# Attention of a gated cross-attention and mixture-of-experts block: its tensor engine products in a written order, and the queries of four groups by quarters, seven products in place of eight

## The chip, the cores and the metric

The kernel runs on one core of a Trainium2 chip. The metric is the device time of one execution in microseconds; the median of three runs is compared. TensorE is called PE here (its weight loads PEld), VectorE DVE, ScalarE ACT, GpSimd POOL; SyncE (SP) issues most of the DMA.

## The reference

The input `x` has 4 x 1024 rows of 256 numbers, the context 4 x 64 rows. All is float32.

```python
def attention(q, k, v):                       # q: normalised x; k, v: the context
    qh = einsum('bld,hdk->hblk', q, w_qs)     # 16 heads of 64
    kh = einsum('bld,hdk->hblk', k, w_ks)
    vh = einsum('bld,hdk->hblk', v, w_vs)
    attn = softmax(einsum('hblk,hbmk->hblm', qh, kh))
    out = einsum('hblm,hbmk->hblk', attn, vh) * qh
    return out.transpose(1, 2, 0, 3).reshape(...) @ w_proj.T + b_proj

def ffn(xt):                                  # 8 experts, the best 2 of each token
    logits = einsum('td,ed->te', xt, gate_w)
    weights = softmax(top_2(logits))          # 0 for the experts not chosen
    h = silu(einsum('td,edf->tef', xt, w1))   # 256 -> 1024
    y = einsum('tef,efd->ted', h, w2)         # 1024 -> 256
    return einsum('ted,te->td', y, weights)

x = x + tanh(g_xattn[0]) * attention(layernorm(x), ctx, ctx)
x = x + tanh(g_ffn[0]) * ffn(layernorm(x))
```

## The kernel before

**Groups and steps.** The 4096 rows are eight groups `g` of 512 (two to a batch, `GB`), a group four tiles of 128 (`T`). The main loop runs over `g` from 0 to 8 and, inside, over four steps `t`. Step `t` of turn `g` works on three groups at once:

- of group `g`: the scores of tile `t` against the keys of the batch (`sc`, 8 products) and the softmax, in `probabilities`. DVE takes the row maximum (`mx`) and subtracts it, ACT exponentiates, DVE sums (`sm`) and inverts, POOL multiplies. One step later `transpose_probabilities` turns the tile with 8 transposes on PE (`pa`), and ACT copies it to `aT`;
- of group `g + 1`: its queries (`pq`), eight pairs of heads spread over the steps by the table `parts`. `queries` multiplies, for each pair, two 128-row blocks of `wq` by 512 columns of the normalised, transposed rows `nT`, and ACT copies the sum from its bank in PSUM to `qT`;
- of group `g - 1`: at step 1 `attend` multiplies attention by values (`po`, four banks for half of the heads), and DVE multiplies by the query in `qT`. At steps 2 and 3 `project` makes the output projection (`pp`, 16 products each), which DVE adds to `x` (line 493).

**Norms.** `ln_stats` and `ln_norm` make the first norm for group `g + 2`: DVE normalises four tiles (line 312), PE turns them (`pt_a`), ACT copies them to `nT`. `add_bias` is on POOL.

**Routing.** After every second group `after` does one part a step for the two groups finished: statistics of the second norm (step 0), norm and logits of the first group (step 1) and of the second (step 2), `route` (step 3), and `place` at step 0 of the next turn. `logits` is a chain: transposes `pt_b`, products `pl` with the gate, a copy to SBUF by DVE, one transpose `pl_t`, a copy to `lg` by DVE (line 520). `route` is some 35 small DVE instructions from `lg` on: comparisons (lines 531 to 536), `chosen` (540), and eight running sums `prior` (543, 544), one for each tile. `place` multiplies `chosen` and `prior` on PE (`prow`, lines 565 and 566); the rows found go to DVE and, through scatters by POOL (`enter`), into a table in DRAM. The rounds belong to groups 0 and 1 (routed at turn 3), 2 and 3 (turn 5), 4 and 5 (turn 7), and 6 and 7 (after the loop).

**Experts.** `run_slots` works through slots of 256 to 384 tokens of one expert: hidden layer (`ph`), output (`py`), a scatter-add into the output. Nine early slots serve groups 0 to 3 and begin inside the loop, by the table `pieces`; the late ones need a table that is made after the last round. `hidden_by_quarters` and `pair_of_blocks` already use seven products for eight in some slots.

**What sets the order.** A scheduler orders each engine's instructions; those given to `pinned` keep the order in which the program states them. Before the change, in attention, that is only the start. Each engine then runs its own list in order and waits at semaphores. PSUM has four single banks (`bank`, pool `ps1`) and two double ones for scores and hidden layers (`ps2`). Large tiles in SBUF come from pools of equal blocks: seven are called `weight`.

Of the kernel before, what the change touches and what calls it, by code (L numbers as in the profile page):

```python
# [15 lines left out]
P = 128  # L16
# [5 lines left out]
def kernel(  # L22
# [140 lines left out]
    load_wk = load_heads(w_ks, "wk", (nc.scalar, nc.sync), "hidden", parts_of)  # L163
    wk, _ = next(load_wk)
# [115 lines left out]

    def ln_stats(groups, name):
# [16 lines left out]
    def ln_norm(g, stats, name):  # L298
# [10 lines left out]
        for t in range(T):  # L309
# [6 lines left out]
            for c in range(NC):  # L316
                turn = nc.tensor.transpose(
                    pt[c][:, t * P : (t + 1) * P], xn[:, c * P : (c + 1) * P], ident
                )
                pinned(turn, first)  # L320
# [50 lines left out]
    def values(ctxT):  # L371

        n = 512 // P
        for b0 in range(0, B, 2):
            for p0 in range(0, NP, n):
                pv = bank(f"pv_{b0}_{p0}")
                for c in range(NC):
                    nc.tensor.matmul(
# [25 lines left out]
    def queries(g, qT, pairs):  # L404
        for p in pairs:
            pq = bank(f"pq_{g}_{p}")
            for c in range(NC):
# [7 lines left out]
                pinned(product, (g, p, c) == (0, 0, 0))  # L415
            nc.scalar.copy(of_pair(qT, p), pq)  # L416

    newest = []

    def probabilities(g, t, qT):  # L420

        sc = ps2.tile([P, NP // 2, 2, 2, M], F32, tag="ps2", name=f"sc_{g}_{t}")
        for p in range(NP):
            nc.tensor.matmul(  # L424
# [23 lines left out]
    def transpose_probabilities(g, t, pr, aT):  # L448
        prv = pr.rearrange("p (i j) m -> p i (j m)", j=2)
        n = 512 // P  # L450
        for p0 in range(0, NP, n):
            pt = bank(f"pa_{g}_{t}_{p0}")
            for i in range(n):
                nc.tensor.transpose(pt[:, i * P : (i + 1) * P], prv[:, p0 + i, :], ident)  # L454
# [4 lines left out]
    def attend(g, pairs, qT, aT):  # L459

        for q in range(pairs[0] // 2, pairs[-1] // 2 + 1):
# [3 lines left out]
            for r in range(2):  # L465
                for j in range(2):
                    half = slice(j * M, (j + 1) * M)
                    i = q * 2 + r
                    nc.tensor.matmul(  # L469
# [10 lines left out]
    def project(g, qT, t0):  # L480

        pp = bank(f"pp_{g}_{t0}").rearrange("p (t d) -> p t d", d=D)
        for i in range(2):
            t = t0 + i
            for p in range(NP):
                nc.tensor.matmul(  # L486
# [16 lines left out]
    def logits(g, lg):  # L503

        pl = bank(f"pl_{g}")[:, :P]
        for c in range(NC):
            for t in range(T):
                nc.tensor.matmul(
# [7 lines left out]
        nc.vector.tensor_copy(lT, pl)  # L516
        pt = bank(f"pl_t_{g}")[:, :P]
        nc.tensor.transpose(pt, lT, ident)
# [3 lines left out]
        )  # L522

# [37 lines left out]
    def place(groups, routing, name):  # L561
# [3 lines left out]
        nc.tensor.matmul(pr, earlier, chosen.rearrange("p t e -> p (t e)"), start=True, stop=False)  # L565
        nc.tensor.matmul(pr, ones, prior.rearrange("p t e -> p (t e)"), start=False, stop=True)
# [50 lines left out]
    def counts(name):  # L617

        pn = bank(f"pn_{name}")[:, :E]
        nc.tensor.matmul(pn, ones, taken, start=True, stop=True)  # L620
# [642 lines left out]
    def finish(g, step):  # L1263

        qT, aT = held[g]
        if step == 1:
            attend(g, range(NP // 2, NP), qT, aT)
        elif step >= 2:
            project(g, qT, (step - 2) * 2)
# [4 lines left out]
    second = {}  # L1274
    entered = 0
    done = in_use = None

    def after(g, step):
# [5 lines left out]
        elif step == 1:  # L1284
            second["logits"] = scores_of([R, E], f"lg_{g}")
            ln_norm(groups[0], second, "b")
            logits(groups[0], second["logits"])
        elif step == 2:
            for h in groups[1:]:
                ln_norm(h, second, "b")  # L1290
                logits(h, second["logits"])
        elif step == 3:
            second["routing"] = route(second["logits"], f"{g}")
# [31 lines left out]
    value_parts = (2, 1, 1, 0)  # L1325
# [3 lines left out]
    queries(0, qTs[0], range(NP - 2, NP))  # L1329
    for g in range(NG + 1):  # L1330
        attention_ends = g == NG
        if g < NG:
# [5 lines left out]
        for t in range(T):  # L1338
            if t == 0 and g >= 2:
                leave(g - 2)  # L1340
            if g < NG:
                pr = probabilities(g, t, qT)
            if last:
                transpose_probabilities(*last)
# [5 lines left out]
            if g and t == 1:  # L1350
                attend(g - 1, range(NP // 2), *held[g - 1])
            for h, pairs in parts[g].items():
                queries(h, qTs[h], pairs[t])
            if 0 <= g - 1 < NG:
                finish(g - 1, t)
            last = (g, t, pr, aT) if g < NG else None
# [3 lines left out]
            if behind >= 0:  # L1360
                after(ends, behind)
            if g == 0 and t == 1:
# [6 lines left out]
            if g + 2 < NG:  # L1369
                if t == 0 and (g + 2) % GB == 0:  # L1370
                    stats = ln_stats(list(range(g + 2, g + 2 + GB)), f"a{g + 2}")
                elif t == 2:
                    ln_norm(g + 2, stats, "a")
                    add_bias(g + 2)
            if g < 2:
                clear(g * T + t, 2 * T)
            for _ in range(pieces[g][t] if g in pieces else 0):
                next(slots)

    leave(NG - 1)  # L1380
    for step in range(2 * T):
        if step == T:
            placing(NG - 1)
        after(NG - 1, step)
        for _ in range((1, 1, 1, 2, 1, 1, 1, 1)[step]):
# [46 lines left out]
```

## Time and profile before

| | |
|---|---|
| median of three runs | 878.94 us (878.19 to 879.98) |
| the profiled execution's own time | 880.53 us |
| its span | 878.7 us |
| mean granted clock of PE | 0.987 |
| busy: PE, PEld | 842.2, 681.6 us |
| busy: DVE, ACT, POOL | 496.0, 244.6, 265.9 us |
| chain that ended last | PE 77%, DVE 12%, waits for issue 4% |
| attention's last projection ends | 442.8 us |

The product of two float32 operands appears as two records on PE, each with a weight load; a transpose is one record. In rows by group, "x256" counts records. "Idle before" is the time for which the engine had nothing to do just before the instruction, and the name behind it is what ended that. Where a row merges several instructions, its duration runs from the first start to the last end.

### The profile page before, as it was taken

Reading aid. Unit: us, or ns where it says so; the run is one execution under the profiler, and the core shown is the slowest. Engines: PE = TensorE matmul, PEld = TensorE weight load, DVE = VectorE, ACT = ScalarE, POOL = GpSimd, SP = SyncE. Lnnn points to the kernel's source line nnn. Section 1 sums busy time; section 2 is a strip of 40 time slices with the busy share of each in tenths; the row PEclk is TensorE's granted clock in tenths of the full one; section 3 lists DMA queues with packets and bytes.
Section 4 is the critical chain, followed back from the end, with each engine's and each line's share of the span. In section 5 each row is a group of like instructions: output and inputs, shape, how many; then the busy total and the mean of one; then the engine's idle time right before and its main releaser. Section 6 shows DMA issues by size and latency. Waiting matters only on the chain.

```text
span 878.7 us, 13306 instructions
## 1 busy us (share of the span) xinstructions
PE 842.2 (96%) x4684; PEld 681.6 (78%) x4684; DVE 496.0 (56%) x1202; ACT 244.6 (28%) x413; POOL 265.9 (30%) x216
## 2 busy tenths in 40 slices
PE   8999999999999999999999699999999999999996
PEld 5555858485767768785888489899999999899995
DVE  4466384679557966862138443665556753546520
ACT  2663242334332323440112012222222221222210
POOL 3052212223721373207224532123222232222132
PEclk9999999999999999999999699999999999999998
DMA  9999999201100055426675668686667675546611
GB/s 197 336 340 341 340 346 340 85 1 60 61 25 1 25 174 163 108 68 189 165 203 147 173 147 215 164 237 140 144 165 178 157 218 133 133 115 176 184 22 37
DMA packets 165032, 141.79 MB, mean 161 GB/s; under 512 B 72685, under 2 KB 159076, under 8 KB 161248
## 3 DMA queue, kind: packets, MB, share of 16 engines
q1 hardware_dynamic: 145456, 118.79, 46.5%
q0 software_dynamic: 12912, 17.11, 10.1%
q10 hardware_dynamic: 6592, 4.98, 1.8%
q8 instruction: 39, 0.64, 0.3%
q14 instruction: 33, 0.27, 0.1%
HBM read 78.73 MB, written 62.46 MB: 161 GB/s over the span
## 4 chain that ended last, share of the span: by engine, by line
PE 77%; DVE 12%; issue 4%; POOL 2%; ACT 2%; DMA 1%; SPq 0%; POOLq 0%; DVEq 0%; ACTq 0%
PE py L1183 20%; PE ph L955 14%; PE ph L1005 11%; PE pp L486 9%; PE pq L408 8%; PE q L1073 5%; PE sc L424 4%; PE pa L454 2%; DVE mx L433 2%; PE po L469 2%; DVE sm L440 1%; DVE pr L435 1%; DVE qT L478 1%; POOL table L606 1%; POOL pr L443 1%
## 5 line engine op out<-in xcount | busy, mean ns | idle before, releaser
L1146 POOL DMA_INDIRECT out_dram<-x,ids x69 | 108.7, 1575 | 306.8 <-DVE x L1161 102.0
L1183 PE MATMUL py<-w,hT 128*128 128x256 f32 (+1 forms) x960 | 186.0, 362 | 0.0
L1183 PEld LDWEIGHTS py<-w,hT 128*128 128x128 f32 (+1 forms) x960 | 160.0, 181 | 21.6 <-issue 1.7
L955 PE MATMUL ph<-xT,w 128*128 128x256 f32 x576 | 135.9, 390 | 7.2 <-issue 7.2
L955 PEld LDWEIGHTS ph<-xT,w 128*128 128x128 f32 x576 | 111.0, 196 | 26.7 <-issue 12.0
L443 POOL TENSOR_TENSOR pr<-pr,sm 128x1024 f32<-128x1024 f32 x32 | 61.4, 1918 | 208.4 <-DVE sm L441 143.0
L408 PE MATMUL pq<-nT_a,wq 128*128 128x512 f32 x256 | 116.1, 597 | 5.7 <-DVE qT L478 3.9
L486 PE MATMUL pp<-wp,qT 128*128 128x256 f32 x512 | 113.5, 379 | 1.3 <-issue 1.3
L486 PEld LDWEIGHTS pp<-wp,qT 128*128 128x128 f32 x512 | 97.0, 190 | 20.0 <-issue 7.4
L408 PEld LDWEIGHTS pq<-nT_a,wq 128*128 128x128 f32 x256 | 46.2, 190 | 58.2 <-issue 44.0
L963 ACT ACTIVATE hT<-ph 128x1024 f32<-128x1024 f32 (+1 forms) x40 | 37.2, 940 | 192.7 <-PE ph L955 119.3
L606 POOL DMA_INDIRECT table<-x,to_row x64 | 62.5, 976 | 42.7 <-DVE x L595 24.8
L424 PEld LDWEIGHTS sc<-keys,qT 128*128 128x128 f32 x512 | 62.6, 192 | 11.2 <-issue 10.8
L424 PE MATMUL sc<-keys,qT 128*128 128x128 f32 x512 | 67.1, 278 | 0.0
L1161 DVE TENSOR_SCALAR x<-py,ids 128x256 f32<-128x256 f32 (+1 forms) x53 | 24.8, 468 | 69.8 <-PE py L1183 63.8
L455 ACT COPY aT<-pa 128x512 f32<-128x512 f32 x64 | 34.7, 592 | 84.1 <-PE pa L454 74.0
L433 DVE TENSOR_REDUCE mx<-sc 128x16 f32<-128x1024 f32 x32 | 39.0, 1219 | 28.0 <-PE sc L424 27.9
L440 DVE TENSOR_REDUCE sm<-pr 128x16 f32<-128x1024 f32 x32 | 39.0, 1219 | 23.9 <-ACT pr L438 21.5
L478 DVE TENSOR_TENSOR qT<-po,qT 128x512 f32<-128x512 f32 x64 | 40.9, 679 | 13.7 <-PE po L469 9.7
L1019 ACT ACTIVATE hT<-hT 128x384 f32<-128x384 f32 (+1 forms) x66 | 33.1, 501 | 51.1 <-DVE hT L1016 48.2
L416 ACT COPY qT<-pq 128x512 f32<-128x512 f32 x64 | 36.5, 581 | 35.3 <-PE pq L408 34.5
L1005 PE MATMUL ph<-x,sa 128*128 128x192 f32 (+1 forms) x264 | 43.6, 314 | 2.0 <-issue 2.0
(278 smaller groups left out, 999.9 us busy)
## 6 DMA issues: line engine op xcount, KB each, us to landing
w<-in_L_ffn_w_dram SPq DMA_DIRECT2D x58, 1024.0 KB
table<-empty SPq DMA_DIRECT2D x8, 5016.0 KB
x<-table SPq DMA_DIRECT2D x116, 64.0 KB
out_dram<-x ACTq DMA_DIRECT2D x8, 512.0 KB
x<-in_x_dram SPq DMA_DIRECT2D x7, 512.0 KB
out_dram<-x,ids POOLq DMA_INDIRECT x69
wq<-in_L_xattn_w_qs_dram SPq DMA_DIRECT2D x4, 256.0 KB
wv<-in_L_xattn_w_vs_dram SPq DMA_DIRECT2D x2, 512.0 KB
```

The lines of the kernel that those rows point to most:

```text
L408: product = nc.tensor.matmul(pq, wq[:, c, p * P : (p + 1) * P], nT[g][:, c, :], start=(c == 0), stop=(c == NC - 1),)
L424: nc.tensor.matmul(sc[:, p // 2, :, p % 2, :], of_pair(qT, p)[:, t * P : (t + 1) * P], kT[g // GB][:, p, :], start=True, stop=True,)
L433: nc.vector.tensor_reduce(mx, scv, AX.X, ALU.max)
L440: nc.vector.tensor_reduce(sm, pr, AX.X, ALU.add)
L443: nc.gpsimd.tensor_tensor(pr, pr, sm.unsqueeze(2).to_broadcast([P, H, M]), ALU.mult).ins,
L478: nc.vector.tensor_tensor(own, po[j], own, ALU.mult)
L486: nc.tensor.matmul(pp[:, i, :], of_pair(qT, p)[:, t * P : (t + 1) * P], wp[:, p, :], start=(p == 0), stop=(p == NP - 1),)
L606: nc.gpsimd.indirect_dma_start(out=table.rearrange("r (u w) -> (r u) w", w=2), out_offset=bass.IndirectOffsetOnAxis(ap=to_row[:, k, i : i ...
L955: nc.tensor.matmul(ph[:, i, :], a[:, c, f * P : (f + 1) * P], xT[:, c, :], start=(c == 0), stop=(c == NC - 1),)
L1005: nc.tensor.matmul(to[:, f, :], left[:, (f0 + f) * P : (f0 + f + 1) * P], right, start=not onto and f == 0, stop=True, skip_group_check=on ...
L1146: rows_added = nc.gpsimd.indirect_dma_start(out=outf.rearrange("n (h d) -> (n h) d", d=w)[:rows_of], out_offset=bass.IndirectOffsetOnAxis( ...
L1183: product = nc.tensor.matmul(py[t][i * m : (i + 1) * m], hT[f // per_tile][:, f % per_tile, t * P : t * P + m], b[:, f, i * w : (i + 1) * ...
```

## The change

**A written order.** `multiply` and `turn` pin every product and transpose of attention from turn 0 on (`steady`), and the loop's body states a new order: the first half of `attend` ahead of the step's scores, the second half after `pa` of the tile before; `pa` itself behind the queries and the projection; the first norm of group `g + 2` at step 3. `logits` becomes a generator in three parts: transposes `pt_b` when it is made, `pl` behind the next step's scores, `pl_t` behind that step's projection.

**Queries by quarters.** For groups 1, 2, 3 and 5, `queries_by_quarters` replaces `queries`. The weights and rows are cut in halves along the contraction and along rows or heads, and seven products of sums replace eight, in two chunks of 14 products of 256 columns (first pairs 0 and 2; a chunk gives two pairs of each half). A chunk uses all four banks, three of them twice. The sums cost four DVE instructions for the weights, once, and four for the rows of each group; five additions a chunk are on DVE, two copies on ACT.

```diff
+    sums_of_wq = block([P, 4, NP // 2 * P], "sums_of_wq", "weight")
+    sums_of_x = block([P, 4, G // 2], "sums_of_x", "weight")
...
+    def multiply(*args, **kwargs):
+        pinned(nc.tensor.matmul(*args, **kwargs), steady)
+    def turn(*args):
+        pinned(nc.tensor.transpose(*args), steady)
...
-                pinned(turn, first)
+                pinned(turned, first or steady)
...
+    QUARTERS = (1, 2, 3, 5)
+    def quarters(h):
+        w = [[wq[:, c, f * NP // 2 * P : (f + 1) * NP // 2 * P] for f in range(2)] for c in range(NC)]
+        x = [[nT[h][:, c, t * G // 2 : (t + 1) * G // 2] for t in range(2)] for c in range(NC)]
+        return w, x
+    def query_weight_sums():
+        w, _ = quarters(0)
+        sa = sums_of_wq
+        for out_, in0, in1, op in (
+            (sa[:, 0], w[0][1], w[1][1], ALU.add),
+            (sa[:, 1], sa[:, 0], w[0][0], ALU.subtract),
+            (sa[:, 2], w[0][0], w[0][1], ALU.subtract),
+            (sa[:, 3], w[1][0], sa[:, 1], ALU.subtract),
+        ):
+            nc.vector.tensor_tensor(out_, in0, in1, op)
+    def query_row_sums(h):
+        _, x = quarters(h)
+        sx = sums_of_x
+        for out_, in0, in1 in (
+            (sx[:, 0], x[0][1], x[0][0]),
+            (sx[:, 1], x[1][1], sx[:, 0]),
+            (sx[:, 2], x[1][1], x[0][1]),
+            (sx[:, 3], x[1][0], sx[:, 1]),
+        ):
+            nc.vector.tensor_tensor(out_, in0, in1, ALU.subtract)
+    def queries_by_quarters(h, qT, f0):
+        w, x = quarters(h)
+        sa, sx = sums_of_wq, sums_of_x
+        per = 2
+        q = [bank(f"pq_{h}_{f0}_{i}").rearrange("p (f n) -> p f n", f=per) for i in range(4)]
+        u2, u3 = (rows.tile([P, per, G // 2], F32, tag="xT", name=f"u_{h}_{f0}_{i}") for i in range(2))
+        to = [[qT[f][:, f0 : f0 + per, t * G // 2 : (t + 1) * G // 2] for t in range(2)] for f in range(2)]
+        def product(to, left, right, onto=False):
+            for f in range(per):
+                multiply(to[:, f, :], left[:, (f0 + f) * P : (f0 + f + 1) * P], right,
+                    start=not onto and f == 0, stop=True, skip_group_check=onto or f > 0)
+        def plus(to, of, other):
+            nc.vector.tensor_tensor(to, of, other, ALU.add)
+        product(q[0], w[0][0], x[0][0])
+        nc.scalar.copy(u2, q[0])
+        product(q[1], sa[:, 1], sx[:, 1])
+        plus(u2, q[1], u2)
+        product(q[2], sa[:, 2], sx[:, 2])
+        plus(u3, q[2], u2)
+        product(q[3], sa[:, 0], sx[:, 0])
+        plus(to[1][1], q[3], u3)
+        product(q[0], w[1][0], x[1][0], True)
+        nc.scalar.copy(to[0][0], q[0])
+        product(q[2], w[1][1], sx[:, 3], True)
+        plus(to[1][0], q[2], u2)
+        product(q[3], sa[:, 3], x[1][1], True)
+        plus(to[0][1], q[3], u2)
...
         nc.vector.tensor_copy(lT, pl)
+        yield
         pt = bank(f"pl_t_{g}")[:, :P]
-        nc.tensor.transpose(pt, lT, ident)
+        turn(pt, lT, ident)
...
-        elif step == 2:
-            for h in groups[1:]:
-                ln_norm(h, second, "b")
-                logits(h, second["logits"])
+        if step in (1, 2):
+            ln_norm(groups[step - 1], second, "b")
+            to_route.append(logits(groups[step - 1], second["logits"]))
...
+    for g in range(NG - 1):
+        if g + 1 in QUARTERS:
+            parts[g] = {g + 1: ([0], [2], [], [])}
-    value_parts = (2, 1, 1, 0)
+    value_parts = (1, 0, 2, 1)
...
+            if g and t == 1:
+                attend_half(g - 1, 0)
             if g < NG:
                 pr = probabilities(g, t, qT)
-            if last:
-                transpose_probabilities(*last)
+            logits_part()
...
             if behind == T:
                 placing(ends)
-            if g and t == 1:
-                attend(g - 1, range(NP // 2), *held[g - 1])
             for h, pairs in parts[g].items():
-                queries(h, qTs[h], pairs[t])
-            if 0 <= g - 1 < NG:
-                finish(g - 1, t)
-            last = (g, t, pr, aT) if g < NG else None
+                if pairs[t]:
+                    ask(h, qTs[h], pairs[t])
+            for _ in range(pieces[g][t] if g in (NG - 1, NG) else 0):
+                next(slots)
+            if g and t >= 2:
+                project(g - 1, held[g - 1][0], (t - 2) * 2)
...
-            if behind >= 0:
+            logits_part()
+            to_route.clear()
+            if 1 <= behind <= 2 and t == 2:
                 after(ends, behind)
+            if g + 2 < NG and t == 3:
+                ln_norm(g + 2, stats, "a")
+                add_bias(g + 2)
+                sum_rows(g + 2)
+            if last:
+                transpose_probabilities(*last)
+            last = (g, t, pr, aT) if g < NG else None
+            if behind >= 0 and not (1 <= behind <= 2 and t == 2):
+                after(ends, behind)
+            if g and t == 1:
+                attend_half(g - 1, 1)
```

`placing` and `prow` keep their place in the program, behind the scores of step 0 and ahead of that step's queries; being products of `multiply`, they are now held there.

## The prediction

> **What bounds the kernel now.** I read the page's first two parts, then the tensor engine (PE) and the vector engine (DVE) in order of time, and then the changed kernel's instruction order on each engine.
>
> ```profile
> PE 842.2 (96%) x4684; PEld 681.6 (78%) x4684; DVE 496.0 (56%) x1202; ACT 244.6 (28%) x413; POOL 265.9 (30%) x216
> L408 PE MATMUL pq<-nT_a,wq 128*128 128x512 f32 x256 | 116.1, 597 | 5.7 <-DVE qT L478 3.9
> ```
>
> PE is busy 96% of the span, and attention (about 30 to 442 us) is no exception: whatever leaves PE there shortens the kernel, and whatever makes PE wait lengthens it. The second row is the query product that the change rewrites; its 5.7 us of idle time is PE waiting behind the attention output `po` for DVE to empty its banks.
>
> Now PE and DVE at the end of group 3, where the first two groups are routed:
>
> ```profile
> 189.41 0.27 PE L518 MATMUL pl_t<-ident,lT 128*128 128x128 f32 x1
> ...
> 191.68 1.98 PE L408 MATMUL pq<-nT_a,wq 128*128 128x512 f32 x4
> 193.50 6.85 PE L486 MATMUL pp<-wp,qT 128*128 128x256 f32 x31
> ...
> 203.06 0.33 PE L565 MATMUL prow<-chosen,earlier 128*128 128x64 f32 x2
> 203.23 0.39 PE L566 MATMUL prow<-prior,ones 128*128 128x64 f32 x2
> ```
> ```profile
> 189.72 0.19 DVE L520 COPY lg<-pl_t 128x32 f32<-128x32 f32 x1
> ...
> 196.60 1.92 DVE L548 TENSOR_TENSOR lg<-lg,top 128x64 f32<-128x64 f32 x1
> ...
> 202.25 0.17 DVE L543 COPY prior<-taken 128x8 f32<-128x8 f32 x1
> ```
>
> The last logits leave PE (`pl_t`) at 189.4. DVE then needs 12.7 us (189.72 to 202.42) until the last copy of `prior`, with one softmax among the routing steps. `prow` reads `prior`, and PE does not reach `prow` before 203.2, because a query product and a whole projection (8.6 us) lie between. So the chain is covered, with less than 1 us over.
>
> **The products.** Four records of 512 columns take 1.72 us in the chain that ended last, 0.429 each; 32 records of 256 columns (`pp`) take 6.91, 0.216 each. A product is two records. A group's queries are 32 x 0.429 = 13.7 us; by quarters they are 2 x 7 x 2 x 2 = 56 records of 256 columns, 12.1. That saves 1.64 us in each of four groups: **-6.6 us**, all of it on PE's path.
>
> **Waits that the new order removes.** The two halves of `po` are now a step apart, with scores and queries between: -5.7 (the row above). Two waits of the transposes `pa` for POOL (0.77 at 50.7, 1.34 at 349.8) get a step of cover: -2.1. In group 8, `po` (1.72 and 0.37 near 406) gets products beside it: -2.1. Together **-9.9**.
>
> **Routing, the large term.** In the changed order the second `pl_t` stands behind the projection, and `prow` right after the next scores, held there. Between them PE has only 8 transposes `pt_a` (0.87, plus 0.6 until their input comes), 8 of `pa` (0.87) and 8 score products (1.8): 4.2 us where 13.6 was. DVE has the same chain: the projection's addition first (0.5 of it left), the steps from `lg` to the last `prior` (12.7; 11.0 if L548 takes 0.22, as it did in the later rounds, instead of 1.92), and in group 4 four row differences, about 1.3 by the 0.32 us of the 128x160 ones. I take the shorter chain: 0.5 + 11.0 + 1.3 = 12.8, less 4.2, is a wait of 8.6 in group 4. Group 6 has no differences but two statistics and aggregations (0.9): 12.4 less 4.2, 8.2. In group 8 there is no softmax; the last round of before took 8.2 (462.3 to 470.5), 1.1 of it other work, so 0.5 + 7.1 = 7.6. The cover there is `pa`, one `ph` and four `py` products, 2.8: a wait of 4.8. Sum **+21.6**. Upper end: the long chain twice, 25. Lower end: routing with nothing between took 7.0 (381.94 to 388.9), so 3.3, 3.3 and 4.7: 11.3. Everything on PE's queue stands behind `prow`: the query chunk, `pa`, `po`, the next scores. That a wait of this kind is taken is seen once in before: L566 at 470.5 sat 0.70 us for `prior` with all expert products behind it.
>
> **The clock.** A long idle time has an aftermath in this trace (stretches with the busy time of PE, PEld, DVE, ACT and POOL, then granted clock, DMA share and GB/s; below them PE's order of time):
>
> ```profile
> 490.00:493.00 3.00, 1.15 (x2) 0.28 (x1) 0.57 (x3) 0.00 (x0) 2.39 (x3) 0.50 0.78 305
> 499.00:502.00 3.00, 3.00 (x8) 2.36 (x7) 2.98 (x25) 0.00 (x0) 1.40 (x1) 0.50 0.77 228
> ```
> ```profile
> 498.07 7.45 PE L955 MATMUL ph<-xT,w 128*128 128x256 f32 x21 [0.62 <-issue]
> ```
>
> From 487 to 498 PE was nearly idle, the granted clock was 0.50, and the next 21 records took 7.45 us where 21 x 0.216 = 4.5 is usual: 2.9 lost. After the smaller waits near 406 (clock 0.59), 30 records took 7.83 instead of 6.5: 1.3 lost. For the waits of groups 4 and 6 I take 2 each, **+4** (0 to 6). [...]
>
> **Quarters on a fuller DVE.** A chunk is 14 products, 6.05 us of PE. ACT copies two banks instead of four. DVE adds five additions from PSUM, 128x512, 0.68 each by row L478, and four row differences a group: about 8.5 us a group on a DVE that is busy 12 to 14 of each 20 us there. The four weight differences fall before the first scores, where DVE sits idle 5.5 us; price 2.7 if that cover were gone. Replay of a chunk from the end of its scores: maximum to 1.2, subtraction to 2.35, first addition to 3.0, second to 3.65, the sum `sm` (it waits for the exponential) to 4.9, third to 5.5. PE needs the third for its last product at 5.2: 0.35 late. Four such steps: 1.4. In groups 0, 2 and 4 the norm's eight statistics are queued ahead of the chunk of step 1. In group 2 DVE is free 4.1 before those scores end, and has the statistics with their aggregations (3.8), four multiplications of `po` (2.5), maximum (1.2), subtraction (1.15), two normalisations (0.8) and two additions (1.25) to do, 10.7: the second addition is there 6.6 after the scores, and the sixth product, which PE reaches at 4.3, waits 2.3. Group 0 has no `po` and waits less, 1.4; I take 1.7, three times: 5.1. Together **+6.5** (0, if DVE keeps up everywhere, to 13).
>
> **Two smaller waits.** `pt_b` moves ahead of the second half of `po`. Its input comes after maximum, subtraction, exponential, sum and reciprocal (4.8) and four normalisations (2.65): 7.6 after the scores, where PE arrives to finish at 5.2. Three times 2.4, less the 2.0 that `pt_b` waits now: **+5** (0 to 7). `pt_a`'s last two transposes wait for a normalisation queued behind the projection's addition, 0.5 in five groups: **+2.5** (0 to 4).
>
> **Costed at nothing.** The two new blocks of sums use up the seven weight buffers, but when the first expert's weights are asked for, both and the first keys are free again; if not, that load would wait for the last query product of group 6. The first experts' tokens land at 339.9 for a product at 343.0; in the replay that margin becomes 1.5 us. The last projection comes 6.9 us of expert work later, but the late table (508.9) and its tokens (transposed by 519.7) precede their first product (539.9) by 20 us. So the shift passes through one for one.
>
> **Sum.** -6.6 - 9.9 + 21.6 + 4 + 6.5 + 5 + 2.5 = +23.1. The profiled execution took 880.5 (span 878.7, 1.8 around it); 903.6 follows. It was 1.6 above the median of the three runs, so: **902**.
>
> **Rivals.** (B) Faster: DVE does not set PE's pace. It keeps up with the chunks and norms (-6.5, -5, -2.5), and `prow` waits only the 11.3 us of the stripped chain, without clock loss (-10.3, -4): 902 - 28.3 = 874. DVE's mean load of 56% speaks for it; the chain of 12.7 us, the fixed order and 19.66 busy us of 20 in the stretch 200 to 220 speak against. It decides from the point where all new waits together stay under 16.5 us. (C) Slower still: DVE's queue is worse than replayed, `prow` at 25 and the chunks at 13: 902 + 3.4 + 6.5 = 912. (D) The stretch from 487 to 498, where PE and DVE both issue one instruction per 1.4 us, depends on where the instructions fall against the table's scatters and goes away: eight idle times before `ph` records, 6.9 in all, and 2.9 of clock, 892. It may as well lengthen. (E) The change does not do what it says: the changed program has 28 products of 256 columns in four groups and `prow` where I say, so nothing is left for this.
>
> **How the numbers follow.** Forecast 0.70, B 0.06, C 0.12, D 0.10, no change 0.02. A measurement of this kernel tells 0.2% (1.8 us) from no change. The range runs from just below D, by what the clock term may be less, to just above C: 890 to 913. It leaves B, no change and the outer ends out. Slower: 0.70 + 0.12 + 0.10 = 0.92.
>
> **What would show it.** Right: PE idle before `prow`, released by DVE `prior`, 8 to 9 us near 203 and again near 311, some 5 near 415, with the clock at 0.5 behind the first two; `pq` records of 256 columns at 0.216; short idle times before `pt_b` and in the chunks, released by DVE. Wrong: no idle time at `prow` (then B), or attention ending less than 10 us later than 442.8.

## The result: 7% slower, two and a half times the predicted loss

The changed kernel takes 938.88 us (937.07 to 941.12, five runs) where the kernel before takes 878.97 beside it: a ratio of 1.068, with an interval of 1.066 to 1.070, or 59.9 us more. The forecast was 902, 23 us more, and its range ended at 913. The profiled execution of the changed kernel took 941.12 us, its span is 939.3, the mean granted clock 0.962 (before 0.987).

In the changed kernel a product that is held has the line of its helper: L287 is `multiply`, L291 `turn`. First the page of its profile, the line of the engines and the row of the queries that still use eight products, then PE's list of waits (in total, times, longest):

```profile
PE 854.0 (91%) x4780; PEld 706.9 (75%) x4780; DVE 535.6 (57%) x1262; ACT 240.6 (26%) x401; POOL 265.2 (28%) x216
L420 PE MATMUL pq<-nT_a,wq 128*128 128x512 f32 x128 | 62.4, 635 | 3.7 <-DVE keys L381 3.7
```
```profile
PE prow L287 <- DVE prior L627: 12.9, 3, 6.2
PE prow L287 <- DVE chosen L624: 8.5, 2, 4.9
PE pt_b L329 <- DVE x L324: 7.9, 6, 1.5
PE ph L1039 <- DVE xT L1012: 7.6, 2, 4.0
PE ph L1039 <- issue: 6.2, 9, 1.0
PE po L287 <- ACT aT L537: 4.7, 7, 3.1
PE py L1267 <- DVE qT L560: 4.5, 1, 4.5
PE pq L420 <- DVE keys L381: 3.7, 1, 3.7
PE pt_a L329 <- DVE xn_a L324: 3.6, 6, 0.7
```

The waits of `prow`, `pt_b` and `pt_a` are those of the prediction. The waits for `keys`, for `aT`, the one of `py` and the longer of the two for `xT` (4.0) are not in it at all; the shorter one (3.6) is part of the third round of routing. The wait of `pq` for `qT` that the row of before showed (3.9) is gone from its place.

Where the time went, by stretches between the first score products of the groups (the last three end at group 8's second `prow`, which is the third round's, at the last projection and at the end). The last two columns are the first two experiments below:

| stretch, us | before | changed | order alone | quarters alone |
|---|---|---|---|---|
| start to first scores | 29.8 | 36.6 | 31.2 | 35.5 |
| turns 0 to 3 | 170.6 | 177.2 | 175.6 | 175.6 |
| turn 4 | 45.2 | 60.6 | 58.4 | 49.0 |
| turn 5 | 49.5 | 51.9 | 53.3 | 49.5 |
| turn 6 | 45.3 | 55.6 | 56.0 | 45.3 |
| turn 7, to the third `prow` | 52.8 | 71.1 | 71.3 | 52.8 |
| to the last projection | 49.6 | 55.4 | 62.0 | 49.4 |
| the rest | 436.0 | 430.9 | 431.5 | 435.9 |

The last row is shorter in the written order because 6.9 us of expert work now stand ahead of the last projection, as the prediction says; without that shift it is 1.9 longer.

The order of time at the end of group 3, PE and then DVE:

```profile
213.81 1.95 PE L287 MATMUL sc<-keys,qT 128*128 128x128 f32 x16
220.62 0.66 PE L287 MATMUL prow<-chosen,earlier 128*128 128x64 f32 x2 [4.86 <-DVE chosen L624]
227.29 0.69 PE L287 MATMUL prow<-prior,ones 128*128 128x64 f32 x2 [6.01 <-DVE prior L627]
227.77 2.02 PE L287 MATMUL pq<-nT_a,wq 128*128 128x256 f32 x4
229.59 4.53 PE L287 MATMUL pq<-sums_of_x,sums_of_wq 128*128 128x256 f32 x12
```
```profile
211.78 0.18 DVE L603 COPY lg<-pl_t 128x32 f32<-128x32 f32 x1
...
214.08 1.15 DVE L615 TENSOR_TENSOR cmp<-lg 128x512 f32<-128x512 f32 x1 [1.35 <-PE pa L291]
...
224.58 1.84 DVE L627 COPY prior<-taken 128x8 f32<-128x8 f32 x1
```

PE waits 10.9 us where 8.6 was predicted. Two things in DVE's rows were not counted. The first comparison (`cmp`) waits 1.35 us after the logits are there, for PE's `pa`. And one copy of eight columns takes 1.84 us instead of 0.17. The clock after it is in the windows (busy PE, PEld, DVE, ACT, POOL; then the granted clock):

```profile
222.00:227.00 5.00, 0.00 (x0) 0.00 (x0) 4.83 (x17) 0.76 (x1) 1.90 (x1) 0.50 0.00 0
228.00:232.00 4.00, 4.00 (x10) 3.19 (x11) 0.69 (x3) 0.58 (x1) 0.00 (x0) 0.50 0.02 4
```

### The profile page after: what moved, and what is told of

Read it like the earlier page. It is cut to its first block, busy times and chain, and to the rows that moved or that the text cites. A ratio compares the mean times of both kernels' runs of the same rounds, so it can differ in the third digit from the quotient of the medians.

```text
span 939.3 us, 13600 instructions
## 1 busy us (share of the span) xinstructions
PE 854.0 (91%) x4780; PEld 706.9 (75%) x4780; DVE 535.6 (57%) x1262; ACT 240.6 (26%) x401; POOL 265.2 (28%) x216
## 5 line engine op out<-in xcount | busy, mean ns | idle before, releaser
L1267 PE MATMUL py<-w,hT 128*128 128x256 f32 (+1 forms) x960 | 190.9, 368 | 4.5 <-DVE qT L560 4.5
L1267 PEld LDWEIGHTS py<-w,hT 128*128 128x128 f32 (+1 forms) x960 | 162.8, 184 | 28.1 <-DVE qT L560 5.4
L1039 PE MATMUL ph<-xT,w 128*128 128x256 f32 x576 | 138.2, 394 | 13.9 <-DVE xT L1012 7.6
L287 PE MATMUL pp<-wp,qT 128*128 128x256 f32 x512 | 113.1, 379 | 0.0
L287 PEld LDWEIGHTS pp<-wp,qT 128*128 128x128 f32 x512 | 96.8, 190 | 15.5 <-issue 2.9
L690 POOL DMA_INDIRECT table<-x,to_row x64 | 62.3, 973 | 62.2 <-DVE x L679 31.2
L287 PEld LDWEIGHTS sc<-keys,qT 128*128 128x128 f32 x512 | 59.8, 192 | 12.3 <-issue 12.3
L420 PE MATMUL pq<-nT_a,wq 128*128 128x512 f32 x128 | 62.4, 635 | 3.7 <-DVE keys L381 3.7
L287 PE MATMUL sc<-keys,qT 128*128 128x128 f32 x512 | 63.8, 278 | 0.0
L420 PEld LDWEIGHTS pq<-nT_a,wq 128*128 128x128 f32 x128 | 24.9, 204 | 31.1 <-issue 30.4
L520 ACT ACTIVATE pr<-pr 128x1024 f32<-128x1024 f32 x32 | 33.8, 1057 | 51.4 <-DVE pr L517 44.3
```

Source lines behind the costliest of these rows:

```text
L287: pinned(nc.tensor.matmul(*args, **kwargs), steady)
L420: product = nc.tensor.matmul(pq, wq[:, c, p * P : (p + 1) * P], nT[g][:, c, :], start=(c == 0), stop=(c == NC - 1),)
L690: nc.gpsimd.indirect_dma_start(out=table.rearrange("r (u w) -> (r u) w", w=2), out_offset=bass.IndirectOffsetOnAxis(ap=to_row[:, k, i : i ...
L1039: nc.tensor.matmul(ph[:, i, :], a[:, c, f * P : (f + 1) * P], xT[:, c, :], start=(c == 0), stop=(c == NC - 1),)
L1267: product = nc.tensor.matmul(py[t][i * m : (i + 1) * m], hT[f // per_tile][:, f % per_tile, t * P : t * P + m], b[:, f, i * w : (i + 1) * ...
```

## The experiments

Each row is told by its distance to the kernel before, run beside it on the same chip: there were five series, and before took 880.2, 877.9, 863.3, 863.6 and 880.3 in them. Where a gain is compared over series, these distances are compared. The changed kernel itself was not run in the two series at 863 (e9 to e12 and e13 to e16), so its distance there is not known: a gain told over that border can be off by some us, and it is the waits in the traces that carry the argument.

| run | over before, us | ratio, interval |
|---|---|---|
| e1 order alone | 59.9 | 1.067 (1.065 to 1.069) |
| e2 quarters alone | 13.4 | 1.014 (1.013 to 1.016) |
| e3 sums on POOL | 59.2 | 1.066 (1.062 to 1.070) |
| e4 `pa` first | 56.6 | 1.065 (1.062 to 1.067) |
| e5 `pl_t` early | 58.0 | 1.066 (1.058 to 1.073) |
| e6 eight scatters | 56.4 | 1.064 (1.060 to 1.069) |
| e7 experts behind | 53.3 | 1.060 (1.055 to 1.064) |
| e8: e3, e5, e6 and e7 together | 50.6 | 1.055 (1.050 to 1.060) |
| e9 own buffers for the routing | 57.7 | 1.065 (1.061 to 1.068) |
| e10: e5 and e9 together | 38.6 | 1.043 (1.040 to 1.046) |
| e11: e8 and e9 together | 26.4 | 1.029 (1.026 to 1.032) |
| e12: e11 without quarters | 21.0 | 1.023 (1.019 to 1.026) |
| e13 stated, not held | 38.2 | 1.042 (1.039 to 1.046) |
| e14: e12 with `pt_b` behind `po` | 20.1 | 1.023 (1.020 to 1.026) |
| e15: e14 with the norm at step 2 | 17.1 | 1.020 (1.017 to 1.023) |
| e16: before with the halves of `po` apart | 10.6 | 1.012 (1.009 to 1.014) |
| e17: e2 with the sums on POOL | 10.0 | 1.010 (1.009 to 1.012) |
| e18: before with group 1 by quarters | 3.7 | 1.004 (1.002 to 1.005) |

### Which part loses

**e1**, the order without the quarters:

```diff
-    QUARTERS = (1, 2, 3, 5)
+    QUARTERS = ()
...
-    query_weight_sums()
```


> The written order without the quarters: all groups ask their queries by eight products a pair, no sums of weights or rows. Theory 1 (most of the loss is in the order: products held behind DVE's routing, and expert tokens that come late) expects about 926: 938.9, less 6.7 of later start, 8 of waits inside the chunks, 1.3 of row differences and some 3 at pt_b, plus 6.6 for the products. The waits for prow stay near 10 us in groups 4 and 6. Rival (the additions of the quarters on DVE make most of the loss): under 900.

**e2**, the kernel before with `queries_by_quarters`, the sums and the new `parts`, in the scheduler's order.


> The kernel before, with the quarters of groups 1, 2, 3 and 5 added and the scheduler's order kept. Theory 1 expects 879 - 6.6 (products) + 6.7 (the weight sums stand ahead of the key copies on DVE here too) + 0 to 8 of waits in the chunks: 879 to 888, and no wait before prow over 1 us. Rival (the quarters make most of the loss): over 905.

The order alone loses as much as both parts together, 59.9; the quarters alone lose 13.4, more than theory 1 of e2 allows and less than its rival (5.7 at the start, 5.0 in turns 0 to 3, 3.8 in turn 4; `prow` waits 1.0 at most in the rounds of turns 4 and 6). So the rival of e1 falls, and the parts don't add up. The table of stretches shows why e1 is not the 926 expected: it is 7.4 us ahead of the changed kernel when group 7 begins, and loses most of that in group 8, where PE stands still beside the table's scatters. Of the timeline of e1:

```profile
474.11 1.22 PE L1267 MATMUL py<-w,hT 128*128 128x256 f32 x2 [10.36 <-issue]
```

**e3**, the four sums of weights by `nc.gpsimd`.


> The changed kernel with the four sums of weights made by POOL instead of DVE; the order on PE, DVE (but for these four) and ACT is the same. Theory 1 (the key copies stood behind the sums, and the sums behind the transfer of wq) expects the first scores near 30 instead of 36.6 and 932, if the 6.7 us pass through to the end. Rival (a later start is absorbed by waits for something with its own time): first scores near 30 and more than 936. If POOL's sums are too slow for the first chunk, a wait of pq for them near 35.

What DVE and PE did at the start of the changed kernel, in order of time:

```profile
15.21 1.29 DVE L448 TENSOR_TENSOR sums_of_wq<-wq 128x512 f32<-128x512 f32 x2 [2.77 <-DMA wq<-in_L_xattn_w_qs_dram]
...
17.86 2.82 DVE L381 COPY keys<-pk 64x256 f32<-64x256 f32 x8
```
```profile
18.88 13.55 PE L420 MATMUL pq<-nT_a,wq 128*128 128x512 f32 x24 [3.72 <-DVE keys L381]
```

The sums stand in DVE's list ahead of the key copies, and wait for the weights' transfer; the copies behind them hold PE's banks; 24 records then take 13.55 us where before took 10.59. The clock tells why (windows of before and of the changed kernel; the third number from the right is the granted clock):

```profile
20.00:40.00 20.00, 20.00 (x65) 10.10 (x65) 8.66 (x26) 10.82 (x20) 1.80 (x1) 1.00 1.13 323
20.00:40.00 20.00, 20.00 (x64) 10.62 (x63) 7.00 (x21) 6.41 (x12) 0.00 (x0) 0.88 1.13 324
```

From 18.1 to 25.0 it was 0.50. So the later start is a wait of 3.7 and 3.0 of slow products behind it. With the sums on POOL the scores start at 30.6, as theory 1 says, but the time is no better (0.7 less over before, within its interval), as the rival says: `py` in group 8 waits 6.7 instead of 4.5, and other turns give the rest back. **e17** repeats it where nothing is held:


> The kernel before with the quarters of four groups, nothing held, and the weight sums on POOL. Quarters alone with the sums on DVE were 13.4 over the kernel before, 5.7 of that at the start. Theory 1 (two separate costs) expects 13.4 - 5.7, so 7 to 9 us over: a ratio of 1.008 to 1.010. Rival (the later start was absorbed, the chunks' waits make it all): 12 or more over, 1.014.

There the scores start 4.4 us earlier than in e2 (31.1 for 35.5), and 3.4 of it reach the end: 10.0, between theory and rival. The start is a separate cost, and what the end sees of it depends on what follows.

### The routing and the buffer it waits for

**e4**, `pa` ahead of the placing:

```diff
             if behind == T:
+                transpose_probabilities(*last)
                 placing(ends)
...
-            if last:
+            if last and behind != T:
                 transpose_probabilities(*last)
```


> The changed kernel with the eight transposes pa of step 0 ahead of the placing in groups 4, 6 and 8, instead of behind the queries. Theory 1 (DVE's of_choice waited 9 us for the softmax buffer that pa gives back, so the table's scatters and the first experts' tokens came 9 us later) expects no such wait, the tokens in time for group 7's first ph (its wait of 3.96 gone, and some of the slow clock behind it), and 0.9 of cover at each prow: 928 to 932. Rival (the tokens are late because the routing is later altogether): only the cover of prow, 2.6, so 936, and ph still waits 3 or more.

**e5**, `pl_t` ahead of the projection: the second `logits_part()` of a step and `to_route.clear()` move up above `project`.


> The changed kernel with one move: the transpose pl_t of the logits stands ahead of the projection instead of behind it, so DVE's routing has the projection (6.9 us of PE) as cover before prow. Theory 1 (prow waits because the written order leaves 4 us of work between the last pl_t and prow) expects the waits for prow to fall from 10.9 to 4 in group 4, from 9.9 to 3 in group 6, to about 0 in group 8, and 3 us less of slow clock behind them: 938.9 - 7 - 7 - 4 - 3, about 918. Rival (DVE reaches the last prior at the same time anyway, because the additions and the softmax in its queue set that): prow waits fall by under 2 each and the time stays over 932.

In e4 DVE's wait of 9 us before `of_choice` is gone and the scatters start 9 us earlier, but those of the next step stand behind that step's softmax on POOL, and the tokens come as late as before (`ph` still waits 3.8 for them): the rival is right. In e5 PE's waits for `prow` are what they were (list of waits of e5):

```profile
PE prow L287 <- DVE prior L627: 13.0, 3, 6.3
...
PE prow L287 <- DVE chosen L624: 8.5, 2, 4.9
```

DVE's timeline of e5 shows what holds them: against group 4's first scores the logits are there 7 us earlier, and the comparison still starts behind `pa`.

```profile
202.27 0.19 DVE L603 COPY lg<-pl_t 128x32 f32<-128x32 f32 x1
...
211.73 1.15 DVE L615 TENSOR_TENSOR cmp<-lg 128x512 f32<-128x512 f32 x1 [1.47 <-PE pa L291]
```

`cmp` is a tile of the softmax pool, which has two buffers. One holds the newest probabilities, the other those that `pa` has yet to turn. In the kernel before `pa` stood right behind the scores; the written order puts it last in the step. **e9** takes that wait away by another buffer, with PE's order as it was:

```diff
-        cmp = soft.tile([P, 2, R, E, E], F32, tag="pr", name=f"cmp_{name}")
-        ahead, same = cmp[:, 0], cmp[:, 1]
+        if name in ("1", "3"):
+            ahead, same = (
+                rows.tile([P, R, E, E], F32, tag="xT", name=f"cmp_{name}_{i}") for i in range(2)
+            )
...
```
(the rounds "1" and "3" are those of turns 3 and 5; `of_choice` likewise), and **e10** adds e5:


> The changed kernel, PE's order untouched: in the rounds of turns 3 and 5 the routing's comparisons (cmp) and of_choice get buffers of another pool (the one called xT) instead of the two softmax buffers. Theory 1 (the comparisons start when pa gives back a softmax buffer, not when the logits are there) expects cmp at the logits' copy, 1.4 us earlier, and of_choice's wait of 9 us on DVE gone: prow waits 1.4 less each, 935 to 936. Rival (the buffers do not matter): 938 to 939.

> The same buffers, and pl_t ahead of the projection. With pl_t alone prow's waits were unchanged at 13.0 and 8.5, since cmp still waited for pa behind the projection. Theory 1 expects cmp right behind the logits' copy, some 8 us earlier, the projection as cover, and of the 10.9 and 9.9 us before prow in groups 4 and 6 at most 2 each, with less slow clock behind: 936 - 16 - 4, about 917; group 8 is as before. Rival (DVE's queue with the projection's addition and the softmax sets the last prior): waits of 6 or more stay, and the time is over 927.

By the distances e9 alone is worth 2.2 and e5 alone 1.9, neither of which can be told from nothing, and both 21.3 (e10 lies 19.1 under e9 in the same series; 38 over before is what its theory 1 expects). The traces say the same: `prow` waits 10.9 and 9.9 us in groups 4 and 6 of the changed kernel and of e5, 10.5 and 9.7 in e9, 0.3 and 0.7 in e10. In e9 `cmp` does start with the logits, but one of the comparisons then takes 2.36 us instead of 0.68, so that not even the 1.4 expected is won. The routing had two locks, and one key opens almost nothing. e10's timelines of DVE and PE:

```profile
204.91 0.19 DVE L603 COPY lg<-pl_t 128x32 f32<-128x32 f32 x1
...
205.98 0.69 DVE L620 TENSOR_TENSOR cmp<-lg 128x512 f32<-128x512 f32 x1
```
```profile
217.52 0.33 PE L287 MATMUL prow<-chosen,earlier 128*128 128x64 f32 x2
218.13 0.43 PE L287 MATMUL prow<-prior,ones 128*128 128x64 f32 x2 [0.27 <-DVE prior L632]
```

### Group 7: experts, tokens, activation tables

The changed kernel's PE and ACT when group 7 begins:

```profile
387.82 6.56 PE L1039 MATMUL ph<-xT,w 128*128 128x256 f32 x16 [3.96 <-DVE xT L1012]
...
398.38 1.95 PE L287 MATMUL po<-aT,vs 64*64 64x512 f32 x16 [3.13 <-ACT aT L537]
...
408.97 0.41 PE L329 MATMUL pt_b<-ident,x 128*128 128x128 f32 x2 [2.33 <-ACT hT L1047]
```
```profile
391.69 1.28 ACT L1047 ACT_TABLE_LOAD   x1 [8.94 <-PE ph L1039]
...
393.59 1.28 ACT L520 ACT_TABLE_LOAD   x1
394.89 1.06 ACT L520 ACTIVATE pr<-pr 128x1024 f32<-128x1024 f32 x1
395.96 1.28 ACT L1047 ACT_TABLE_LOAD   x1
```

The expert's hidden layer now stands ahead of `pa`, and waits for tokens whose scatters end later in a longer turn. Behind it ACT changes its table for `silu`, for the exponential and back, 1.28 us each, before it copies `aT`; `po` waits for that. Ten tables are loaded in this turn, seven before the change.

**e6**, `6 *` becomes `8 *` in the two bounds of the scatters a step. **e7**, group 7's `next(slots)` at the end of the step. **e8**, these with e5 and e3.


> The changed kernel with eight table scatters a step instead of six, so a round's 16 are issued in two steps instead of three. Theory 1 (the first experts' tokens are read behind the last scatter, and the scatters of a step stand behind that step's softmax on POOL; the moving of prow and the longer turn pushed the third step's past the need) expects the tokens one step earlier, some 9 us; group 7's wait of ph for xT (3.96) and the slow clock behind it (3.1) go: 932. Rival (the time that is won here is given back in group 8, as in the runs before): ph's wait gone, but over 936.

> The changed kernel with group 7's expert products at the end of each step, as in the kernel before, instead of ahead of the projection. Theory 1 (on ACT the silu of the experts, with its table load, came ahead of the softmax's exponential and the copies aT, so po and pt_b waited for ACT and DVE in group 7) expects po's wait for aT (3.1) and pt_b's for hT (2.3) in group 7 to go and ph's first wait to fall from 4.0 to about 3: 932 to 934. Rival (ACT changes its table the same number of times, the waits move to other products): over 936.

> The three moves together, and the weight sums on POOL: pl_t ahead of the projection, eight scatters a step, group 7's experts at the end of the step. Theory 1 expects the sum: 938.9 - 20 - 7 - 5.5, and 0 to 5 for the earlier start: 901 to 907. Rival (what is won ahead of group 8 is lost there to stretches in which all engines stand still beside the table's scatters): attention's end moves by less than 20 of these and the time stays over 915.

e6 takes the first wait for tokens away and 4.0 us out of the turn; 3.5 reach the end, between what theory and rival say. e7 gains 6.6, as theory 1 says: `po`'s wait for `aT` falls from 4.7 to 1.3 in all and the first `ph` waits 3.0, while `pt_b` waits 6.2 for its rows in that turn, where it waited 1.5 (and 2.3 for ACT). e8 gains 9.3, near the sum of e6 and e7 (10.1): e5 adds nothing without the buffers, and the rival's "over 915" came true, not the 901 to 907.

**e11** adds the buffers to e8, and **e12** drops the quarters from e11.


> All that is mended so far: own buffers, pl_t ahead of the projection, eight scatters a step, group 7's experts at the end of the step, weight sums on POOL. Theory 1: 928.5 - 16 - 4, about 908. Rival (given back in groups 7 and 8): over 918.

> The same as the run of five (all queries by eight products a pair, so no sums at all). Up to group 5 the quarters cost 3.8 more in waits than their 6.6 of products in the written order; theory 1 expects this to show here, since no other wait hides it: 2 to 5 below the run of five, about 905. Rival (the quarters gain once the routing is out of the way): 3 or more above it.

e11 is 26.4 over before, where 29 was expected: the buffers bring 24.2 on top of e8, measured in another series. Without the quarters it is 5.4 less, in the same series. So where the routing is out of the way and the weight sums are not on DVE, quarters placed as they are here still cost more in waits than their products save: until the last projection PE is idle 36.3 us in e11 and 27.8 in e12.

### What is left of the order

**e13**: `steady = False`, all else as in the changed kernel.


> The changed kernel with the new sequence of statements and the quarters, but no product of attention held to it: the scheduler may move them, as before the change. Theory 1 (the loss is made by holding products behind DVE's work) expects no prow wait over 2 us and the 13 us that the quarters alone cost, with 0 to 10 for the sequence: 13 to 23 us over the kernel before. Rival (the sequence of statements alone does it, since the scheduler follows it): 40 us or more over.

38.2: near the rival's 40, not the 13 to 23 of theory 1. With the products free, 38 of the 60 remain (told over series), where the quarters alone lost 13; the difference comes with the sequence of the statements. `prow` still waits 12.9 in turns 4 and 6 (3.7 to 5.0 at a time), for the same rows of DVE.

**e14** and **e15**: in e12 `attend_half(g - 1, 1)` moves ahead of `after`, then the norm to step 2.


> The run of five without quarters (21 us over the kernel before), with the transposes pt_b of step 1 behind the second half of po instead of ahead of it. Theory 1 (pt_b stands there 12.7 us for DVE's normalised rows) expects 2.8 less in each of groups 3 and 5, 3 of the 6.2 in group 7, so 8 to 9 less: 12 to 13 us over. Rival (po's output then stops the next scores or queries, as in the kernel before): 18 or more over.

> The same, and the first norm of group g + 2 at step 2 instead of 3, as in the kernel before. Theory 1 (pt_a's last two transposes wait for a normalisation queued behind the projection's addition, 7.0 us in six places, 2.2 of it in the rounds of routing) expects 4 to 6 less than the run with pt_b moved: 7 to 9 us over the kernel before. Rival (at step 2 the same queue stands behind the other half of the projection): no less than that run.

e14 gains 0.9, nothing that can be told, as its rival says: `pt_b` no longer waits for its rows in groups 3 and 5 (2.8 each in e12), but 5.2 us in all for DVE to empty the banks of the `po` now ahead of it. e15 gains 3.0 on that, less than its theory 1 expects.

**e16** puts one part of the change alone into the kernel before: the first `attend` of step 1 moves ahead of `probabilities`, nothing is held.


> The kernel before with one part of the change alone, and nothing held: the first half of po ahead of the scores of step 1 instead of behind them. Theory 1 (the prediction's 5.7 us of po and pq waiting for DVE to empty po's banks are real, and a distance between the halves removes them) expects 3 to 6 us less than the kernel before: a ratio of 0.993 to 0.997. Rival (other products wait for the same banks instead): within 1 us of the kernel before, or slower.

It is 10.6 slower. The waits of `pq` and `po` for banks (6.5) are nearly gone, but of PE's timeline:

```profile
174.74 0.33 PE L317 MATMUL pt_b<-ident,x 128*128 128x128 f32 x1 [2.55 <-DVE qT L478]
```

that wait was 0.72 before; `pt_b` waits 8.0 in all where it waited 2.0, and `po` 2.9 for ACT. The banks are emptied no sooner; another product finds them full. In turns 0 to 6 PE is idle 9.5 us where it was 8.4, and yet they take 7.8 us longer. Part of the rest is the clock: behind the wait of 2.55 it was 0.68 from 174.7 to 180.0, where behind the shorter waits of before, from 171.9 to 177.0, it was 1.00; from 273 to 279 it was 0.72.

**e18**, group 1 alone by quarters in the kernel before, sums on POOL:


> The same with group 1 alone by quarters; its chunks fall in the turn of group 0, where no attention output, routing or projection is on DVE. Theory 1 (a chunk gains its 0.8 us where DVE is free, and loses where DVE has a turn's other work) expects 1.6 for the products and up to 2 for fewer bank waits, less 1 of waits inside the chunks: 0.5 to 3 us under the kernel before, a ratio of 0.997 to 0.999. Rival (the chunk's chain of additions costs more than it saves everywhere): 1 or more over.

Its chunks run without a wait, 6.05 us each as predicted, and still it is 3.7 slower, though not for the reason that the rival gives. The two chunks stand in steps 0 and 1, where before had query products in every step. In the steps that they no longer fill, the scores of two steps follow each other and `pa` waits for the softmax:

```profile
56.92 3.07 PE L496 MATMUL sc<-keys,qT 128*128 128x128 f32 x26
64.34 1.97 PE L526 MATMUL pa<-ident,pr 128*128 128x128 f32 x8 [4.36 <-POOL pr L515]
```

From 64.0 to 67.0, behind this wait, the granted clock was 0.50; the eight `pa` take 1.97 where eight take 1.04 at 53.16. The same waits of `pa` are in e2 (6.3 us in all). Chunks spread over other steps were not tried. So none of these versions beats the kernel before.

## Why the prediction was right in direction and wrong in size

Slower was right, and the largest term, the routing, was right in cause and nearly in size. Three steps failed: the clock was priced behind two waits alone, two things that cost 6.8 and some 12 us stood under "costed at nothing", and the waits counted as removed came back elsewhere.

The traces give the account by cause. Until the last projection ends, PE is idle 17.9 us in before and 65.5 in the changed kernel, 47.6 more, where the prediction's waits sum to 25.7. Of its busy time 3.4 us lie at a granted clock of 0.50 in before (407.9 to 411.3) and 38.6 in the changed kernel (eight stretches, from 18.1 to 478.9). Taking half of such time as lost, an estimate from that clock, that is 17.6 more, where the prediction has 4. The remaining busy time is the same within 0.5, since 6.6 saved on products and 6.9 of expert work moved ahead nearly cancel. So of the 37 us too few, some 22 are idle time, some 14 the clock, and 2 lie behind the last projection.

**Waits before `prow` (21.6, bounds 11 to 25): right.** 10.9 and 9.9 in groups 4 and 6, and 4.0 in group 8, where 3.6 of it falls on the `ph` ahead of `prow`: its copy `xT` stands in DVE's list behind the comparisons of the routing. That is 24.7, near the upper bound. The term was 3 short: the prediction chose the chain with the short L548 (0.22), but one instruction of DVE is 1.7 longer in groups 4 and 6 too, only not the same one; and `cmp` waits for `pa` (1.35 and 0.47), which the prediction did not see. e10 shows the cover to be the cause, with the softmax buffer as a second lock.

**Clock (4): the step was mis-sized, 17.6 where 4 was forecast.** Behind the two waits that it names the term is right, 4.5 (6.55 for sixteen records where four and twelve take 3.78, so 2.8; 8.56 where 6.87 was, so 1.7). But shorter waits had the same aftermath: 3.0 at the start behind a wait of 3.7, 2.9 behind group 7's first `ph` (4.0), 1.9 behind group 8's `py` (4.5), and some behind `pt_b` and the third round. Not every wait of this length had it: behind `po` at 398.4 (3.13) the clock was 1.00, and behind `pt_b` it was 0.50 from 182.3 and 1.00 from 295.8, both times after waits of 1.30 and 1.47. Behind the first wait at `prow` the trace shows 0.50 until 233, 5.8 us of work.

**Chunks (6.5), `pt_b` (5), `pt_a` (2.5): right in kind.** The waits in the chunks sum to 8.0 (`sums_of_x` 1.7, `u` 3.2, `qT` 1.8 and 1.3), those of `pt_b` grew from 2.0 to 10.2 (2.3 of it for ACT's `hT`), those of `pt_a` are 3.6.

**Costed at nothing: wrong, 6.8.** "The four weight differences fall before the first scores, where DVE sits idle 5.5 us" looked at DVE's time and not at its list. They were queued ahead of copies that PE needs, and wait for a transfer. Even the price of 2.7 that the prediction gave for lost cover was too small. e3 takes 6.0 of the 6.8 back at the start; the rest is also in e1.

**Costed at nothing: wrong, some 12.** "That margin becomes 1.5 us" for the first tokens. The margin went to a wait of 3.96, and the new place of the experts' products was never walked through on ACT: its tables, `aT` and `pt_b`. Turn 7 lost 18.2 us, 1.3 of it expert work that is only moved ahead; the terms of the prediction that fall there come to 5.1 (`prow` 4.8, a third of `pt_b` 1.7, less 1.3 of `pa`). e6 and e7 show 10 of the rest.

**Waits removed (-9.9): wrong in part.** In the changed kernel the waits for `po`'s banks did leave their places, but 5.9 us for the same products of DVE (`qT`) came back, 1.3 in a chunk and 4.5 at `py` in group 8. In the scheduler's order the edit alone costs 10.6 (e16). The prediction removed a wait without asking which product finds the banks next.

**Products (-6.6): the chunk is as short as predicted** where nothing holds it, but e18 shows that a step emptied of query products no longer covers the softmax, and e12 that the four groups together lose.

By stretches, of the 37 us too few 6.8 lie at the start, 13 in turn 7, 3 behind it, and 15 in turns 0 to 6 (34.8 measured, 20.1 in the terms there): of these 4 at `prow`, 4 in the other waits, 3 in the clock, and the rest in products that run a little longer than counted, which was not taken apart. Rival D did not come true in this run: PE waits for issue at 549 to 560 as it did at 487 to 498. Left open: what the remaining 17 us of e15 consist of (the longest waits are those of `pt_b`, 11.2 in all, and of `pt_a`, 4.3), and why group 8 loses between 0 and 10 us to standstills beside the scatters.

## What to carry to other kernels

An instruction that "falls into idle time" has a place in an in-order list: look at what it waits for and who is queued behind it. A wait has a price beyond its length when the clock falls behind it (here 1.9 to 3.0 us behind waits of 3.7 to 4.5): count the slow products behind every wait of a few us that the change makes, not behind the longest alone. A wait for a bank or a buffer is not removed by moving its victim; name the next instruction that asks for the same one, and for a chain look at every lock on it (here logits and softmax buffer), since opening one alone shows nothing. When an order is written by hand, walk it through on every engine whose queue it passes, ACT's table changes (1.28 us each here) included.

## What the runs showed of the hardware

**DVE and POOL.** The long copy above, 224.58 to 226.42, lies under POOL's softmax product of 224.49 to 226.39. In before L548 took 1.92 from 196.60 and from 291.25, while POOL's products ran until 198.44 and 293.09, and L642 1.93 from 304.44, while POOL ran from 304.40 for 1.90. Each of these four ends 0.03 to 0.08 us after POOL's product. Other instructions of DVE keep their time there: the maximum `mx` took 1.23 from 348.45 in before, under POOL's product of 347.80 to 349.70, and 1.22 is its median. That POOL's product holds the four up is an inference from these rows, which no run tested. The delay shows as a long instruction, not as idle time, and falls on another instruction when the order changes: in the changed kernel the step of L548 took 0.22 at 217.70.

**Two levels of one kernel.** The kernel before took 878 to 880 us in three series and 863 in two, and the last series at 880 was on the chip of the same number (11) as the two at 863; so it is not shown to be a matter of the chip. In the traces of the 863 series the waits of `ph` for issue are gone (6 to 11 us in the others), the stretch behind the last projection takes 419 to 421 us instead of 431 in kernels of the written order, and group 8's `py` doesn't wait. What makes those standstills was not shown.
